# A two-layer mixer kernel: PSUM evictions issued half a state later, six state buffers in place of five, both halves of the step sizes in one PSUM slot

## The chip, the cores and the metric

The kernel runs on one core of one Trainium2 chip. A core has TensorE (PE in the profile; its weight loads are shown as PEld), VectorE (DVE), ScalarE (ACT), GpSimd (POOL) and SyncE (SP), which here issues the DMAs. The metric is the device time of one execution in microseconds; lower is better. The output must equal the reference's.

## The reference, cut to what matters

Two layers work on x of shape (4, 64, 64, 128). The costliest part is the selective scan of the first layer: four directions, 256 channels, 16 states for each channel, 4096 positions, four images.

```python
def step(h, xs):                       # over 4096 positions
    ut, dt, bt, ct = xs
    dA = jnp.exp(dt[..., None] * A)
    h = dA * h + (dt * ut)[..., None] * bt[:, :, None, :]
    y = jnp.einsum('bkdn,bkn->bkd', h, ct)
    return (h, y)
...
# layer 0
x = x + _L0_conv_ref(_ln_c(x), ...)    # projection, 3x3 convolution, selective scan, gate
t = t + _L0_ffn_ref(_ln_t(t), ...)     # 64 experts, each takes its top 8 positions
# layer 1
x = x + _L1_conv_ref(_ln_c(x), ...)    # self, row sum and column sum, three projections
t = t + _L1_ffn_ref(_ln_t(t), ...)     # long causal convolutions with 16 filters, and 3 taps
```

`dt` is softplus of a projection with rank 8, which the kernel calls the step sizes.

## The kernel before, in words

All data are fp32. The scan is cut into chunks: for each of 4 images and 4 directions, 8 chunks of 512 positions, 128 chunks in all. In a chunk each of the 16 states n is one step of the main loop, so there are 2048 steps s, each on tiles of 128 channels x 2 halves x 512 positions. The loop is software-pipelined. In step s of the program:

- SP loads the rows B and C of state s+5, spread over all partitions (`bc`, 6 buffers, L1355);
- ScalarE makes `da` = exp(dl * A) of state s+3, one instruction for each half (L1365, 5 buffers);
- VectorE makes `db` = du * B (L1392) and runs two scans into `hh` of state s (L1398, 5 buffers);
- GpSimd multiplies `hh` of state s-1 by C in place (L1408) and keeps the last column in `hst` (L1407);
- TensorE transposes `hh` of state s-2 into `y` and adds it up over the 16 states in PSUM (L1434, eight matmuls).

Once per chunk come the step sizes of the next chunk, `step_sizes`, one piece in each step from n = 1 on: load `dts` and `xc`; for each half take a PSUM tile `dt_ps`, project (L1280), and read it twice on ScalarE, into `ex` (L1282) and `dl` (L1283); then a softplus on ScalarE and GpSimd, which ends with `dl` (L1297) and `dx` = dl * x (L1299). At the end of the chunk ScalarE copies `dx` into PSUM as `du` (L1346), which has one buffer, so that the next chunk's `db` waits for this copy.

PSUM has 8 banks. `du`, `db` and `y` take 2 each; the last 2 are the side work's, either as two slots of one bank (`bank`, most of the time) or as one slot of two banks (`pair`, while `convolve` runs beside the recurrence; `bank` then takes half of it).

All other work of the kernel is side work, written as generators that yield a weight after each piece. Beside the recurrence of image b runs: for b = 0 the preparation of the other images, the gates and the filters' spectra; for b > 0 the end of the first layer for image b-1 (`after_scans`), the experts and the second layer's sums (`experts_and_sums`), the first transform of the long convolution (`to_slots`) and a part of the convolution itself (`convolve`: matmuls `cv_ps`, copied to SBUF as `y`, then 16 matmuls into `zq_ps`). `deal` takes pieces until their weights have reached what is due, twice in each step (in the middle and at the end of TensorE's transposes), except in the steps n = 2 and 3 of a chunk. It asks that the pieces' instructions come behind the step's own instruction on their engine. The final order on each engine is decided by a scheduler, which may move an instruction past others as long as dependencies and these requests hold. `pipelined` runs the stages of such a generator in the manner of a software pipeline: stage k of item g in the round g + k, an empty stage (None) is a round of waiting.

After the recurrence comes a tail: the side work of the last image together with most of the convolution, with all 8 banks as slots. There an eviction goes to VectorE and ScalarE in turn; beside the recurrence it is always a ScalarE copy (`evict`, L240).

Of the kernel before, what the change touches and what calls it, by code (L numbers as in the profile page):

```python
# [10 lines left out]
F32 = mybir.dt.float32  # L11
AF = mybir.ActivationFunctionType
# [5 lines left out]
P = 128  # L18
# [60 lines left out]
def kernel(  # L79
# [124 lines left out]

    side = {"tail": False}

    def slots(ones, twos):
        if "pool" in side:  # L210
# [2 lines left out]
        for name, n in (("ones", ones), ("twos", twos)):  # L213
            side[name] = n and side["pool"].enter_context(
                tc.tile_pool(name=f"side_{name}", bufs=n, space=PSUM)
            )

    def bank(shape, name):

        if side["ones"]:  # L220
            return side["ones"].tile(shape, F32, name=name, tag="ps")
        n = int(np.prod(shape[1:]))
        ap = pair(name)[0 : shape[0], 0, 0:n]
        if len(shape) == 2:
            return ap
        sizes = {f"d{i}": d for i, d in enumerate(shape[1:])}
        names = " ".join(sizes)
        return ap.rearrange(f"p ({names}) -> p {names}", **sizes)

    def pair(name):  # L230

        return side["twos"].tile([P, 2, 512], F32, name=name, tag="ps2")

    def evict(dst, src):
# [27 lines left out]
    def pipelined(n, *stages):  # L262


        for step in range(n + len(stages) - 1):
            for s in reversed(range(len(stages))):
                if 0 <= step - s < n and stages[s]:
                    stages[s][1](step - s)
                    yield stages[s][0]

    def norm_sums(pool, t, n, width, eps):

# [39 lines left out]
    def transposed(dst, src, n, name):  # L312

        ps = bank([P, n, P], name)
        for q in range(n):
            nc.tensor.transpose(ps[:, q, :], src[:, q, :], ident)
        evict(dst, ps.rearrange("c q p -> c (q p)"))

    def sigmoid_of(pool, ps, h):

# [14 lines left out]
    def before_scans(b):  # L335
# [6 lines left out]
        with tc.tile_pool(name="pa", bufs=1) as pa:  # L342
# [78 lines left out]
            with tc.tile_pool(name="pa_x", bufs=3) as px:  # L421
                xs, sts = {}, {}

                def load_x(i):
                    xs[i] = px.tile([P, 2, SC], F32, name="xc_x", bufs=5)
                    c = i % NSC
                    nc.sync.dma_start(
                        xs[i],
                        xc_d[b][i // NSC, :, :, c * SC : (c + 1) * SC].rearrange("h p l -> p h l"),
                    )  # L430

                def project(i):
# [6 lines left out]
                    evict(sts[i], ps)  # L439
# [12 lines left out]

                yield from pipelined(2 * NSC, (0.7, load_x), None, None, (1.8, project), None, (2.5, put_bc))
# [31 lines left out]
    def after_scans(b):  # L485

        with tc.tile_pool(name="po", bufs=2) as po:
# [19 lines left out]
            def add(g):  # L507
                ps = bank([P, 2, DI], "yk_ps")
                for k in range(K):
                    nc.tensor.matmul(ps, ident, yk.pop((g, k)), start=(k == 0), stop=(k == K - 1))  # L510
                y[g] = po.tile([P, 2, DI], F32, name="y", bufs=8)
                evict(y[g], ps)

            def sums(g):
                st[g] = norm_sums(po, y[g], 2, DI, eps5)
# [25 lines left out]
            def project(g):  # L541
                ps = bank([P, 2, C], "pr_ps")
                for q in range(2):
                    for h in range(2):
                        nc.tensor.matmul(
                            ps[:, q, :],
                            yT[g][:, h, q * P : (q + 1) * P],
                            w_out_t[:, h, :],
                            start=(h == 0),
                            stop=(h == 1),  # L550
                        )
                pr[g] = po.tile([P, 2, C], F32, name="pr")
                evict(pr[g], ps)

            yield from pipelined(
                16,
# [133 lines left out]
    def experts_and_sums(b):  # L690

        with tc.tile_pool(name="mk", bufs=1) as kp:
# [203 lines left out]
            with tc.tile_pool(name="l1", bufs=2) as lp:  # L896
# [4 lines left out]
                with tc.tile_pool(name="l1a", bufs=2) as la:  # L901
# [5 lines left out]
                    def scatter(g):  # L907
                        ps = bank([P, 4, C], "sc_ps")
                        for q in range(4):
                            t0 = 512 * g + q * P  # L910
                            nc.tensor.matmul(
                                ps[:, q, :], pT[:, t0 : t0 + P], outE, start=True, stop=True
                            )
                        sc[g] = la.tile([P, 4, C], F32, name="sc")
                        evict(sc[g], ps)

                    def sums(g):
                        st[g] = norm_sums(la, x4(g), 4, C, eps6)
# [32 lines left out]
                with tc.tile_pool(name="l1b", bufs=2) as lb:  # L951
# [5 lines left out]
                    def mix(g):  # L957
# [18 lines left out]
                        evict(zs[g], ps)  # L976

                    def sums2(g):
                        st2[g] = norm_sums(lb, x2g(g), 2, C, eps5)
# [15 lines left out]
                    def regress(g):  # L995
# [14 lines left out]
                        nc.scalar.activation(ar[g], ps, AF.Identity, scale=wseg[:, sg : sg + 1])  # L1010

                    yield from pipelined(
                        16,
# [21 lines left out]
    def to_slots(b):  # L1035

        with tc.tile_pool(name="fu", bufs=3) as fp:
            ub, uo = {}, {}

            def load(g):  # L1040

                ub[g] = fp.tile([NB, 4, 2, C], F32, name="ub")
                nc.sync.dma_start(
                    ub[g].rearrange("j t a c -> j (t a) c"),
                    u_d[b].rearrange("(j t) c -> j t c", j=NB)[:, 8 * g : 8 * g + 8, :],
                )

            def turn(g):
                uo[g] = fp.tile([P, 4, 2, C], F32, name="uo")
                for a in range(2):  # L1050
                    ps = bank([P, 4, C], "fu_ps")
                    nc.tensor.matmul(ps, fu_t, ub[g][:, :, a, :], start=True, stop=True)  # L1052
                    evict(uo[g][:, :, a, :], ps)

            def put(g):
                for r in range(2):
# [1 line left out]
                        ud[b][:, r, 4 * g : 4 * g + 4], uo[g][r * NQ : (r + 1) * NQ]  # L1058
                    )

            yield from pipelined(BS // 4, (0.5, load), (2.0, turn), (1.0, put))

    def convolve(groups, pool=None):

# [3 lines left out]
        with tc.tile_pool(name="cv", bufs=2) if pool is None else nullcontext(pool) as cp:  # L1068
# [30 lines left out]
            for i, (b, G, kq, e) in enumerate(parts):  # L1099
# [7 lines left out]
                for a in range(2):  # L1107

                    off = 1 - a if e == 1 else 0
                    for p in range(2):  # L1110
# [14 lines left out]
                                evict(to[:, q], pq[q])  # L1125
                            yield 0.0
                        else:
                            evict(to, ps)
                            yield 4.0
                if e == 0:  # L1130
                    continue
# [52 lines left out]
    def from_slots(b):  # L1184

        with tc.tile_pool(name="gi", bufs=3) as gp:
# [11 lines left out]
                    )  # L1198

            def turn(g):  # L1200
                xr[g] = gp.tile([NB, 4, 2, C], F32, name="xr3", bufs=4)
# [4 lines left out]
                iv[g] = gp.tile([NB, 4, 2, C], F32, name="iv")  # L1206
                for a in range(2):
                    ps = bank([NB, 4, C], "gi_ps")
                    nc.tensor.matmul(ps, gi_t, zb[g][:, :, a, :], start=True, stop=True)  # L1209
                    nc.scalar.activation(iv[g][:, :, a, :], ps, AF.Identity, scale=wpj[0:NB, :])  # L1210

            def add(g):

# [6 lines left out]
                    xr[g].rearrange("j t a c -> j (t a) c"),  # L1220
                )

            yield from pipelined(BS // 4, (0.7, load), (2.5, turn), (3.0, add), (0.5, put))

    def run(pieces):
        for _ in pieces:
# [23 lines left out]
    with ExitStack() as c0:  # L1250
# [11 lines left out]
        def step_sizes(b, k, ci):  # L1262


            dl = pb.tile([P, 2, SC], F32, name="dl", bufs=3)
            dx = pb.tile([P, 2, SC], F32, name="dx", bufs=1)
            xc = pb.tile([P, 2, SC], F32, name="xc")

            def pieces():
                cs = slice(ci * SC, (ci + 1) * SC)  # L1270
                dts = pb.tile([R, SC], F32, name="dts")
                nc.sync.dma_start(dts, dts_d[b][k, :, cs])
                nc.sync.dma_start(xc, xc_d[b][k % 2, :, :, cs].rearrange("h p l -> p h l"))
                yield
                ex = pb.tile([P, 2, SC], F32, name="ex", bufs=1)
                w = pb.tile([P, 2, SC], F32, name="w", bufs=1)

                for h in range(2):
                    ps = bank([P, SC], "dt_ps")
                    nc.tensor.matmul(ps, dtw[:, k, h * P : (h + 1) * P], dts, start=True, stop=True)  # L1280
                    bias = dtb[:, k, h : h + 1]
                    nc.scalar.activation(ex[:, h, :], ps, AF.Abs, bias=bias)  # L1282
                    nc.scalar.activation(dl[:, h, :], ps, AF.Relu, bias=bias)  # L1283
                    yield
                nc.scalar.activation(ex, ex, AF.Exp, scale=-1.0)
                yield
                nc.scalar.activation(w, ex, AF.Identity, bias=1.0)
# [28 lines left out]
        def deal(*behind):  # L1316


            if i % (K * NSC) < FIRST or s >= total or s % N in BUSY:
                return  # L1320
            start = len(traced)
            share["due"] += WEIGHT[chunks[i][0]] / ((K * NSC - FIRST) * (N - len(BUSY)) * 2)
            while share["made"] < share["due"]:
                share["made"] += next(share["pieces"], 1e9)
# [23 lines left out]
        for s in range(-5, total + 2):  # L1348
# [23 lines left out]
            if 0 <= s < total:  # L1372
                b, k, step, _ = chunks[i]
                n = s % N
                if n == 0:
                    if k == 0 and step == 0:
                        y_d[b] = dram.tile([K, L, DI], F32, name=f"y_d{b}")
                        if b > 0:
                            run(share["pieces"])
                        share = {"pieces": beside(b), "made": 0.0, "due": 0.0}  # L1380
                    hsts[i] = pb.tile([P, 2, N], F32, name="hst") if step == 0 else hsts[i - 1]
                    if i == 0:
                        into_psum(0)
                if i + 1 < len(chunks):
# [7 lines left out]
                nc.vector.tensor_mul(db, dus[i], bcs[s][:, 0:1, :].to_broadcast([P, 2, SC]))  # L1392
                for h in range(2):
# [183 lines left out]
```

## Time and profile before

| | us |
|---|---|
| median of three runs | 11290.32 (11284.48 to 11290.91) |
| the profiled execution | 11279.9 |
| its span, first to last instruction | 11278.1 |
| first `db` of the recurrence starts | 299.9 |
| last scan starts | 9087.1 |

| engine, busy in the span | us | share |
|---|---|---|
| TensorE matmuls | 8435.7 | 75% |
| VectorE | 8146.8 | 72% |
| GpSimd | 7262.7 | 64% |
| ScalarE | 6181.0 | 55% |

Costs of one instruction: `db` 1232 ns, a scan 1267 ns (1208 at the start of a direction), an exponential 716 ns, the product by C 2359 ns, a transposing matmul of `y` 322 ns as recorded (they overlap), a `dt_ps` matmul 822 ns. In the profile a name such as "hh<-da,hst,db" is output and inputs, L1398 the line; an idle time stands with the instruction that ended it. The shares of a whole span are averages over two quite different stages, so that the stretches have to be looked at one by one.

### The profile page before, as it was taken

The page shows a single profiled execution, that of the slowest core. Times are in us where ns is not written, and L with a number is a line of the kernel's source. Part 1 is how long each engine was busy: PE and PEld are TensorE (multiplying, and loading weights), DVE is VectorE, ACT ScalarE, POOL GpSimd, SP SyncE. Part 2 cuts the span into 40 slices and gives each one's busy share as a digit, 9 for nine tenths or more (in the row PEclk, how much of TensorE's full clock was granted, in tenths as well). Part 3 has the DMA queues.
Part 4 walks back from the last instruction along what each step waited for, and adds up shares of the span by engine and source line. Part 5 has one row for each costly group of instructions (what it writes and reads, how often), then busy time and mean ns, then how long its engine had stood idle before and what let it go on. Part 6 is the DMA issues. An engine that isn't in the chain of part 4 may idle for free. (4 is left out here: it accounts for less than half of the span.)

```text
span 11278.1 us, 117105 instructions
## 1 busy us (share of the span) xinstructions
PE 8435.7 (75%) x34656; PEld 4819.2 (43%) x34656; DVE 8146.8 (72%) x7046; ACT 6181.0 (55%) x12043; POOL 7262.7 (64%) x6518
## 2 busy tenths in 40 slices
PE   6677676556776777757766777576677789999998
PEld 2444443334453444444543344455344444355443
DVE  0898888887987999879878898798698932222222
ACT  4757575657466565664655566657455544124222
POOL 1888787888787877787867788888687821001001
PEclk9687787757777888878778788787788899999999
DMA  2565656566655666657565566575666664553555
GB/s 97 164 202 186 203 170 202 192 188 201 226 178 178 197 180 193 204 163 249 166 174 167 167 192 207 167 264 155 171 198 181 183 163 122 151 137 95 140 131 120
DMA packets 901457, 1980.14 MB, mean 176 GB/s; under 512 B 101562, under 2 KB 415578, under 8 KB 899290
## 3 DMA queue, kind: packets, MB, share of 16 engines
q1 hardware_dynamic: 900826, 1972.65, 58.2%
q8 instruction: 283, 4.64, 0.2%
q14 instruction: 348, 2.85, 0.1%
HBM read 1766.77 MB, written 205.52 MB: 175 GB/s over the span
## 5 line engine op out<-in xcount | busy, mean ns | idle before, releaser
L1408 POOL TENSOR_TENSOR hh<-hh,bc 128x1024 f32<-128x1024 f32 x2048 | 4829.8, 2359 | 434.2 <-DVE hh L1398 192.2
L1398 DVE TENSOR_TENSOR_SCAN hh<-da,hst,db 128x512 f32<-128x512 f32 x3584 | 4392.9, 1267 | 675.6 <-PE y L1434 297.9
L1365 ACT ACTIVATE da<-dl,aneg 128x512 f32<-128x512 f32 x4096 | 2766.3, 716 | 2084.4 <-DVE hh L1398 1998.3
L1434 PE MATMUL y<-ident,hh 128*128 128x128 f32 x16384 | 2808.2, 322 | 1214.8 <-POOL hh L1408 1095.7
L1434 PEld LDWEIGHTS y<-ident,hh 128*128 128x128 f32 x16384 | 2293.9, 167 | 2637.0 <-POOL hh L1408 1424.9
L1392 DVE TENSOR_TENSOR db<-du,bc 128x1024 f32<-128x1024 f32 x2048 | 2523.5, 1232 | 633.6 <-ACT du L1346 547.7
L1116 PE MATMUL cv_ps<-slab,us 64*128 64x512 f32 x4096 | 1197.3, 691 | 533.5 <-ACT y L240 277.8
L240 ACT COPY y<-cv_ps 128x512 f32<-128x512 f32 (+1 forms) x1024 | 754.3, 741 | 667.8 <-PE cv_ps L1116 638.0
L1407 POOL COPY hst<-hh 128x2 f32<-128x2 f32 x1792 | 338.9, 189 | 1123.6 <-DVE hh L1398 980.0
L1137 PE MATMUL zq_ps<-y,me 128*128 128x512 f32 x2048 | 1000.1, 609 | 49.0 <-ACT y L240 43.3
L1137 PE MATMUL zq_ps<-y,mo 128*128 128x512 f32 x2048 | 969.3, 597 | 0.0
L238 DVE COPY y<-cv_ps 128x512 f32<-128x512 f32 x640 | 441.5, 691 | 561.9 <-PE cv_ps L1116 511.8
L1116 PEld LDWEIGHTS cv_ps<-slab,us 64*128 64x128 f32 x4096 | 407.7, 206 | 1002.5 <-ACT y L240 369.3
L1153 POOL TENSOR_TENSOR zt<-zt,zt 128x512 f32<-128x512 f32 x64 | 81.2, 1268 | 996.2 <-DVE zt L238 536.5
L1398 DVE TENSOR_TENSOR_SCAN hh<-da,db 128x512 f32<-128x512 f32 x512 | 597.1, 1208 | 113.4 <-PE y L1434 70.8
L388 PE MATMUL cv_ps<-xh,diag 128*128 128x512 f32 x1152 | 534.7, 607 | 0.3 <-ACT xh L381 0.2
L1137 PEld LDWEIGHTS zq_ps<-y,me 128*128 128x128 f32 x2048 | 352.5, 193 | 382.2 <-issue 262.1
L1280 PE MATMUL dt_ps<-dts,dtw 8*128 8x512 f32 x512 | 371.4, 822 | 175.5 <-ACT dl L1283 48.3
L1137 PEld LDWEIGHTS zq_ps<-y,mo 128*128 128x128 f32 x2048 | 356.3, 191 | 316.6 <-issue 313.9
L1292 POOL TENSOR_TENSOR ex<-ex,dx 128x1024 f32<-128x1024 f32 x128 | 302.6, 2364 | 169.2 <-ACT dx L1289 169.0
L238 DVE COPY zt<-zq_ps 128x512 f32<-128x512 f32 x39 | 26.9, 691 | 529.0 <-PE zq_ps L1137 523.3
L510 PE MATMUL yk_ps<-yk,ident 128*128 128x512 f32 x512 | 275.2, 677 | 85.3 <-DMA yk<-y_d 34.0
(222 smaller groups left out, 8705.0 us busy)
## 6 DMA issues: line engine op xcount, KB each, us to landing
bc<-bc_d SPq DMA_DIRECT2D x2048, 512.0 KB
slab<-hd SPq DMA_DIRECT2D x1024, 256.0 KB
xc<-xc_d SPq DMA_DIRECT2D x128, 512.0 KB
y_d<-ys SPq DMA_DIRECT2D x128, 512.0 KB
w1t<-in_w_dram SPq DMA_DIRECT2D x128, 512.0 KB
w2t<-in_w_dram SPq DMA_DIRECT2D x256, 256.0 KB
xc_x<-xc_d SPq DMA_DIRECT2D x64, 512.0 KB
yk<-y_d SPq DMA_DIRECT2D x128, 256.0 KB
```

What stands on the lines that cost most here:

```text
L238: nc.vector.tensor_copy(dst, src)
L240: nc.scalar.copy(dst, src)
L388: nc.tensor.matmul(ps, diag[:, h, t, :], xh[:, 8 * g + dy : 8 * g + dy + 8, dx : dx + W], start=(t == 0), stop=(t == 8),)
L1116: nc.tensor.matmul(pq[q].rearrange("p (r k t) -> p r k t", r=2, t=BS), us[b, G][rows, p, a if e == 0 else 1 - a, :], slab[i][rows, p, :, : ...
L1137: nc.tensor.matmul(z, (me, mo)[e][:, KQ * kq + k, :], ys[e][:, :, :, :, k, :].rearrange("p a q r t -> p (a q r) t"), start=(e == 0 and k = ...
L1280: nc.tensor.matmul(ps, dtw[:, k, h * P : (h + 1) * P], dts, start=True, stop=True)
L1365: i_act = nc.scalar.activation(das[t][:, h, :], sizes[t // N][0][:, h, :], AF.Exp, scale=aneg[:, tk, h, t % N : t % N + 1],)
L1392: nc.vector.tensor_mul(db, dus[i], bcs[s][:, 0:1, :].to_broadcast([P, 2, SC]))
L1398: i_dve = nc.vector.tensor_tensor_scan(o, d0, d1, init, ALU.mult, ALU.add)
L1407: nc.gpsimd.tensor_copy(hsts[t // N][:, :, t % N], hhs[t][:, :, last])
L1408: i_pool = nc.gpsimd.tensor_mul(hhs[t], hhs[t], bcs.pop(t)[:, 1:2, :].to_broadcast([P, 2, SC]))
L1434: i_pe = nc.tensor.matmul(ys[c][:, q, h, :], hhs[t][:, h, q * P : (q + 1) * P], ident, is_transpose=True, start=(n == 0 and k > 0 and q % ...
```

## The change

Five edits.

- While the recurrence runs (`side["deals"]` is set), `evict_soon` doesn't issue the copy out of PSUM but puts it in a list, `soon`. `settle` issues what is in it: at the start of each `deal`, before a pair is taken, before the step sizes take their slot, at the end of a round of `pipelined` whose weights are under 6, and, all but the last, before a bank is taken. Ten kinds of eviction use it, among them those of `cv_ps`, `fu_ps`, `gi_ps`, `yk_ps`, `pr_ps`, `sc_ps`, `z_ps` and `ar_ps`; those of `zq_ps`, `zt_ps`, `pk_ps` and the reads of `cv_ps` in the first layer do not.
- `hh` has six buffers.
- While PSUM is a pair, both halves of `dt_ps` go to the two banks of one slot: two matmuls in one piece, four reads in the next.
- `to_slots` and `from_slots` get empty stages (between load and turn, turn and put, turn and add), and one buffer more for `ub`, `uo`, `iv` and `xr3`.
- `dl` has two buffers in place of three, `dts` one in place of two.

```diff
-    side = {"tail": False}
+    side = {"tail": False, "deals": False}
...
+    soon = []
+
+    def settle(leave=0):
+        while len(soon) > leave:
+            soon.pop(0)()
+
+    def evict_soon(work):
+        if side["deals"]:
+            soon.append(work)
+        else:
+            work()
+
     def bank(shape, name):

         if side["ones"]:
+            settle(1)
             return side["ones"].tile(shape, F32, name=name, tag="ps")
...
     def pair(name):

+        settle()
         return side["twos"].tile([P, 2, 512], F32, name=name, tag="ps2")
...
         for step in range(n + len(stages) - 1):
+            whole = 0.0
             for s in reversed(range(len(stages))):
                 if 0 <= step - s < n and stages[s]:
                     stages[s][1](step - s)
+                    whole += stages[s][0]
                     yield stages[s][0]
+
+            if whole < 6.0:
+                settle()
+        settle()
...
-        evict(dst, ps.rearrange("c q p -> c (q p)"))
+        evict_soon(lambda: evict(dst, ps.rearrange("c q p -> c (q p)")))
...
-                ub[g] = fp.tile([NB, 4, 2, C], F32, name="ub")
+                ub[g] = fp.tile([NB, 4, 2, C], F32, name="ub", bufs=4)
...
-                uo[g] = fp.tile([P, 4, 2, C], F32, name="uo")
+                uo[g] = fp.tile([P, 4, 2, C], F32, name="uo", bufs=4)
...
-                    evict(uo[g][:, :, a, :], ps)
+                    evict_soon(lambda ps=ps, a=a: evict(uo[g][:, :, a, :], ps))
...
-            yield from pipelined(BS // 4, (0.5, load), (2.0, turn), (1.0, put))
+            yield from pipelined(BS // 4, (0.5, load), None, (2.0, turn), None, (1.0, put))
...
-                            evict(to, ps)
+                            evict_soon(lambda to=to, ps=ps: evict(to, ps))
                             yield 4.0
...
-            yield from pipelined(BS // 4, (0.7, load), (2.5, turn), (3.0, add), (0.5, put))
+            yield from pipelined(BS // 4, (0.7, load), (2.5, turn), None, (3.0, add), (0.5, put))
...
-            dl = pb.tile([P, 2, SC], F32, name="dl", bufs=3)
+            dl = pb.tile([P, 2, SC], F32, name="dl")
...
-                dts = pb.tile([R, SC], F32, name="dts")
+                dts = pb.tile([R, SC], F32, name="dts", bufs=1)
...
-                for h in range(2):
-                    ps = bank([P, SC], "dt_ps")
+                settle()
+
+                def project(h, ps):
                     nc.tensor.matmul(ps, dtw[:, k, h * P : (h + 1) * P], dts, start=True, stop=True)
+
+                def read(h, ps):
                     bias = dtb[:, k, h : h + 1]
                     nc.scalar.activation(ex[:, h, :], ps, AF.Abs, bias=bias)
                     nc.scalar.activation(dl[:, h, :], ps, AF.Relu, bias=bias)
-                    yield
+
+                if side["ones"]:
+                    for h in range(2):
+                        ps = bank([P, SC], "dt_ps")
+                        project(h, ps)
+                        read(h, ps)
+                        yield
+                else:
+                    ps = pair("dt_ps")
+                    for work in (project, read):
+                        for h in range(2):
+                            work(h, ps[:, h])
+                        yield
...
             start = len(traced)
+            settle()
             share["due"] += WEIGHT[chunks[i][0]] / ((K * NSC - FIRST) * (N - len(BUSY)) * 2)
...
+        side["deals"] = True
...
                             run(share["pieces"])
+                            settle()
...
-                hhs[s] = pb.tile([P, 2, SC], F32, name="hh", bufs=5)
+                hhs[s] = pb.tile([P, 2, SC], F32, name="hh", bufs=6)
...
         run(share["pieces"])
+        settle()
+        side["deals"] = False
         side.pop("pool").close()
```

More of the change, by code (lines that the diff above doesn't have):

```diff
@@ L438, in project @@
                     sts[i] = px.tile([104, SC], F32, name="xd_st", bufs=4)
-                    evict(sts[i], ps)
+                    evict_soon(lambda: evict(sts[i], ps))
                 def put_bc(i):
@@ L511, in add @@
                 y[g] = po.tile([P, 2, DI], F32, name="y", bufs=8)
-                evict(y[g], ps)
+                evict_soon(lambda: evict(y[g], ps))
             def sums(g):
@@ L552, in project @@
                 pr[g] = po.tile([P, 2, C], F32, name="pr")
-                evict(pr[g], ps)
+                evict_soon(lambda: evict(pr[g], ps))
             yield from pipelined(
@@ L914, in scatter @@
                         sc[g] = la.tile([P, 4, C], F32, name="sc")
-                        evict(sc[g], ps)
+                        evict_soon(lambda: evict(sc[g], ps))
                     def sums(g):
@@ L975, in mix @@
                         zs[g] = lb.tile([P, 2, C], F32, name="zs")
-                        evict(zs[g], ps)
+                        evict_soon(lambda: evict(zs[g], ps))
                     def sums2(g):
@@ L1009, in regress @@
                         ar[g] = lb.tile([P, 2, C], F32, name="ar")
-                        nc.scalar.activation(ar[g], ps, AF.Identity, scale=wseg[:, sg : sg + 1])
+                        evict_soon(
+                            lambda: nc.scalar.activation(
+                                ar[g], ps, AF.Identity, scale=wseg[:, sg : sg + 1]
+                            )
+                        )
                     yield from pipelined(
@@ L1200, in turn @@
             def turn(g):
-                xr[g] = gp.tile([NB, 4, 2, C], F32, name="xr3", bufs=4)
+                xr[g] = gp.tile([NB, 4, 2, C], F32, name="xr3", bufs=5)
                 nc.sync.dma_start(
@@ L1205, in turn @@
                 )
-                iv[g] = gp.tile([NB, 4, 2, C], F32, name="iv")
+                iv[g] = gp.tile([NB, 4, 2, C], F32, name="iv", bufs=4)
                 for a in range(2):
@@ L1209, in turn @@
                     nc.tensor.matmul(ps, gi_t, zb[g][:, :, a, :], start=True, stop=True)
-                    nc.scalar.activation(iv[g][:, :, a, :], ps, AF.Identity, scale=wpj[0:NB, :])
+                    evict_soon(
+                        lambda ps=ps, a=a: nc.scalar.activation(
+                            iv[g][:, :, a, :], ps, AF.Identity, scale=wpj[0:NB, :]
+                        )
+                    )
             def add(g):
```

## The prediction

> **What bounds the kernel now.** I read the busy slices first, then the busy time by stretch, then VectorE's waits inside the long stage, then single waits in the timeline.
>
> ```profile
> PE   6677676556776777757766777576677789999998
> ...
> DVE  0898888887987999879878898798698932222222
> ...
> PEclk9687787757777888878778788787788899999999
> ...
> 300.00:2430.00 2130.00, 1432.55 (x5652) 893.47 (x5652) 1887.06 (x1557) 1376.30 (x2557) 1760.29 (x1386) 0.75 0.58 188
> ...
> 9088.00:11278.00 2190.00, 2113.19 (x7106) 942.18 (x7104) 541.68 (x781) 688.87 (x1625) 260.75 (x532) 0.98 0.54 132
> ```
>
> Two regimes: from 300 to 9088 us the recurrence runs with VectorE the busiest (1887 of 2130 us in its first quarter, the columns being PE, weight loads, DVE, ACT, POOL); the last 2190 us are TensorE's, 2113 busy. The floor of the first regime is one state on VectorE:
>
> ```profile
> 6268.81 2.45 DVE L1398 TENSOR_TENSOR_SCAN hh<-da,hst,db 128x512 f32<-128x512 f32 x2
> 6271.29 1.23 DVE L1392 TENSOR_TENSOR db<-du,bc 128x1024 f32<-128x1024 f32 x1
> 6272.66 2.45 DVE L1398 TENSOR_TENSOR_SCAN hh<-da,hst,db 128x512 f32<-128x512 f32 x2
> ```
>
> Scans of one state start 3.85 us after those of the state before. 2048 x 3.85 = 7885 us, but the stage takes 8788, so some 900 us are lost. About 100 of them are other VectorE work (maxima, sums); the rest is waiting, and one view names it:
>
> ```profile
> DVE db L1392 <- ACT du L1346: 547.7, 50, 289.5
> DVE hh L1398 <- PE y L1434: 368.7, 115, 17.5
> DVE hh L1398 <- ACT da L1365: 56.8, 31, 5.7
> ...
> PE cv_ps L1116 <- ACT y L240: 262.5, 158, 8.6
> ...
> PE fu_ps L1052 <- DMA ub<-u_d: 55.3, 7, 20.1
> ...
> PE dt_ps L1280 <- ACT dl L1283: 48.3, 32, 10.9
> ```
>
> (total us, times, longest.) The 289.5 is the start-up; the other 258 us of du fall at chunk boundaries. The second line is a full ring of hh tiles: scan s cannot write until TensorE has transposed state s-5. The last three are why TensorE is late: it stands before a PSUM slot that ScalarE has not emptied, or a late load. One boundary shows it whole:
>
> ```profile
> 6267.66 0.60 PE L1434 MATMUL y<-ident,hh 128*128 128x128 f32 x4
> 6273.15 2.07 PE L1280 MATMUL dt_ps<-dts,dtw 8*128 8x512 f32 x2 [4.89 <-ACT zt L240]
> 6276.57 2.07 PE L1280 MATMUL dt_ps<-dts,dtw 8*128 8x512 f32 x2 [1.36 <-DMA slab<-hd]
> 6280.00 2.15 PE L1116 MATMUL cv_ps<-slab,us 64*128 64x512 f32 x4 [1.36 <-DMA bc<-bc_d]
> 6282.08 1.97 PE L1434 MATMUL y<-ident,hh 128*128 128x128 f32 x8
> ...
> 6302.39 1.23 DVE L1392 TENSOR_TENSOR db<-du,bc 128x1024 f32<-128x1024 f32 x1 [11.84 <-ACT du L1346]
> ```
>
> dt_ps waits for zt's eviction, the second half for both reads of the first, the convolution for the reads of the second; no transpose of the recurrence starts for 14 us. (The DMA names are misattributed: both matmuls follow the end of a dl read by 0.05 us.)
>
> **What the Trainium skill says.** "PSUM — Partial Sum Buffer", section Engine vs sequencer instructions: the queues of ScalarE, VectorE and GpSimd are strict FIFO and matmuls start in program order. The lines above agree: transposes whose hh was ready sat behind dt_ps. "Perfetto Trace Analysis", section Optimization Strategy: a repeated gap on the engine that should be full can mean too few buffers for the next tile. The 115 hh waits agree in kind. "TensorE: Matmul & The Clock Gate", section HAM oscillation: idle gaps over about 3.4 us put TensorE back to half clock. The trace agrees: four fu_ps records take 3.75 us after a 9.42 us wait and 1.98 us in a stretch without one; so a TensorE wait taken away also makes the next work faster.
>
> **The change, part by part**, against the profiled execution (11279.9 us; span 11278.1), which lies 10 us under the median 11290.3.
>
> *Sixth hh tile.* It lets VectorE run one state further ahead of TensorE. A stretch of late TensorE then costs one state, 3.85 us, less, once per stretch, as the ring must refill in between. I followed each VectorE wait over 0.15 us back to its cause: 405 us belong to transposes (some under other names than the 368.7), in 74 stretches when waits at most five states apart are put together. Capped at 3.85 each they sum to 192 us. Not all comes back: where TensorE stays late until the chunk ends, du is late next, and where ScalarE is the pace (norm phases: the 16 states from 2726 us take 92 us instead of 61.7, ScalarE 73 of them busy, and the scans wait for da) the time is due anyway. I take 60%: 115 us; bounds 40 and 192.
>
> *Evictions half a state later.* No instruction is added; a copy keeps its 0.57 to 1.0 us. On ScalarE it now stands in the next deal's place. The orders of the two programs, compared engine by engine, show how little that is: a scheduler had already moved the evictions behind later exponentials; 153 of some 2050 state groups differ on TensorE, 19 on VectorE, 750 on ScalarE, mostly by one place or one state, and the neighbours of du are the same at half of the boundaries. Gain: ScalarE no longer stands at a matmul not yet done (164 us before cv_ps copies in the stage) while exponentials queue behind it; those have four states in hand, so little reaches VectorE. Loss: the PSUM slot is held longer, by up to two exponentials (2 x 0.716 = 1.43 us), and TensorE's next side matmul, the transposes behind it and then hh wait. On time, the exponentials of a state end about 1.4 us after the scan that frees them and a pair's copy 1.0 later, 2.4 us; TensorE reaches its slot after POOL's 2.36 us product and four transposes, about 3 us. So it just fits. Net +10 us of gain; bounds -150 and +40.
>
> *Both halves of dt in one slot.* Only where PSUM is one pair (the convolution's 48 chunks). It removes the wait between the halves: 1.36 us in the lines above, 48.3 us in all on TensorE, and brings the second dt one or two states forward in 38 of them. In eight slow chunks (80 to 87) dt stands behind a whole zq sum, is not moved, and du is late by up to 11.8 us; there the dl chain gains about 1.35 us each, 11 us. Elsewhere most of it is hidden by the sixth tile: 6 us. Together 17; bounds 0 and 60.
>
> *Loads two steps ahead in to_slots.* The SP queue had ud stores, which wait for evictions, ahead of later ub loads (6 stores held it 11.4 us at 5717). Now four ub loads go first. Of 55 us of ub waits the first of each of three runs stays, about 35; 15 of the rest reach VectorE. Bounds 0 and 40.
>
> *dl 3 to 2, dts 2 to 1 buffers.* The old dl has been read ten states before it is rewritten, dts almost a chunk before: 0.
>
> *du.* Where VectorE no longer stops for hh, it reaches the chunk's end with TensorE later than before, and a du behind an eviction is then late: I give back 27 us (bounds 0 and 80), the next wait in line.
>
> *Tail.* Evictions are immediate there, the matmuls the same in number and TensorE 96% busy: 0, within 15.
>
> Sum: 115 + 10 + 17 + 15 - 27 = 130 us. 11279.9 - 130 = 11150 for that execution, 11160 for the median.
>
> **Rivals.**
> *The reordering does little and the sixth tile hands over to du (15%).* For: half the du neighbours are unchanged and 258 us of du already wait. Against: after nearly all long hh waits near a chunk's end no du wait follows. Time: 192 x 0.2 = 38 less du's 27: about 11280.
> *The gains chain (8%).* TensorE, interrupted less, stays at full clock (0.75 to 0.80 now), its lateness vanishes and all 405 us less the 150 of rate-bound stretches go: 11290 - 255 = 11035.
> *Slower: the held slot (17%).* In the convolution one pair serves every cv_ps, dt_ps and zq sum. Of 384 pair evictions half are issued at a state's end and now fall behind the next two exponentials: 192 x 1.43 = 275 us of TensorE time. It decides from the point where ScalarE reaches an eviction later than TensorE its slot, by the above with only 0.6 us of margin; then TensorE's lateness exceeds what one more hh tile (3.85 us per stretch) hides, and the gains of 130 shrink to the other phases' half. 11290 + 275 - 65 - a third of the 275 hidden (92) = about 11410. For: TensorE already waits 262.5 us for y copies. Against: where TensorE is late the exponentials have already been run.
>
> **How the numbers follow.** 60% for the forecast, 11160, its own range 11080 to 11235. Faster by over 0.2% (23 us, about what a measurement here tells from none): 0.60 + 0.08 + 0.06 of the first rival = 0.74; within: 0.09; slower: 0.17. The range 11040 to 11340 leaves out a third of the chained case and most of the upper half of the slower one.
>
> **What would show it.** Waits of the scan for y: from 368.7 to about 250, fewer than 70; TensorE's dt_ps wait for dl in the convolution gone; du (without start-up) at 230 to 290; ub waits near 35; chunks of the second convolution nearer 61.7 us; 9088 moves to about 8960 and the tail stays near 2190. Wrong if cv_ps's wait for y copies grows past 400 us, or the hh waits stay above 330.

## The result, and the profile after

| | before | after |
|---|---|---|
| median (runs) | 11289.81 us (4) | 11197.33 us (4; 11189.8 to 11203.89) |
| ratio after / before, 95% interval | | 0.992 [0.9907, 0.9932] |
| profiled execution | 11279.9 us | 11189.8 us |
| first `db` to the end of the last scan | 299.9 to 9088.3 | 297.0 to 9007.2 |
| from there to the end of the span | 2189.8 us | 2180.8 us |

The change makes the kernel 92 us faster, most of it in the recurrence (78 us of the 90 between the two profiled executions; the tail is 9 us shorter). Busy slices of the page, and busy time in its first quarter and in the tail (columns as before: PE, weight loads, DVE, ACT, POOL, clock, DMA share, GB/s):

```profile
PE   6677676546766777657677776576677789999999
...
DVE  0898988887887999879878898798699933222222
...
PEclk9787777757776888778778887687788899999999
...
300.00:2430.00 2130.00, 1406.59 (x5652) 882.42 (x5650) 1886.03 (x1557) 1375.90 (x2556) 1762.08 (x1387) 0.75 0.58 189
9008.00:11188.00 2180.00, 2111.85 (x7100) 940.43 (x7100) 541.18 (x780) 688.77 (x1625) 260.09 (x532) 0.99 0.53 133
```

The picture has the same two regimes, and VectorE is as busy in the first quarter as it was (1886 against 1887 us): its work is unchanged, and its waits must have gone. The waits of VectorE and then of TensorE between 300 and 9030 us (total us, times, longest) show which:

```profile
DVE db L1440 <- ACT du L1393: 340.6, 55, 16.8
DVE hh L1446 <- PE y L1482: 176.3, 49, 19.8
DVE hh L1446 <- ACT da L1412: 79.5, 40, 6.3
...
DVE db L1440 <- DMA bc<-bc_d: 34.7, 23, 7.9
...
PE cv_ps L1142 <- ACT y L256: 284.9, 166, 8.7
...
PE fu_ps L1078 <- DMA ub<-u_d: 43.0, 3, 19.3
```

The window leaves out the start-up, so that 340.6 stands against 258 of before. The full ring of hh cost 368.7 us and now costs 176.3: 192 us less. But du rose by 82 us, da by 23 and bc by 22 (from 12.6 us in 6 waits). Some 127 of the 192 us have changed their name and are still paid. The order of the first two lines has turned round.

By stretch: the convolution's 48 chunks went from 3120.2 to 3069.5 us, the other chunks with side work of b > 0 from 3534.1 to 3505.9, those of the first image not at all (2134.2 and 2134.7).

The boundary that the prediction showed lies here in the changed kernel (timelines of TensorE, ScalarE, GpSimd and VectorE; start, duration):

```profile
6220.06 3.78 PE L1311 MATMUL dt_ps<-dts,dtw 8*128 8x512 f32 x4 [4.89 <-ACT zt L256]
6226.35 2.15 PE L1142 MATMUL cv_ps<-slab,us 64*128 64x512 f32 x4 [2.51 <-ACT dl L1316]
...
6242.04 1.33 ACT L1412 ACTIVATE da<-dl,aneg 128x512 f32<-128x512 f32 x2 [8.67 <-POOL dl L1342]
6243.28 0.99 ACT L256 COPY y<-cv_ps 128x1024 f32<-128x1024 f32 x1
6244.17 2.56 ACT L1412 ACTIVATE da<-dl,aneg 128x512 f32<-128x512 f32 x4
6246.63 0.99 ACT L256 COPY y<-cv_ps 128x1024 f32<-128x1024 f32 x1
6247.53 0.59 ACT L1393 COPY du<-dx 128x512 f32<-128x512 f32 x1
6248.05 0.72 ACT L1412 ACTIVATE da<-dl,aneg 128x512 f32<-128x512 f32 x1
6248.67 0.58 ACT L1393 COPY du<-dx 128x512 f32<-128x512 f32 x1
...
6242.09 2.35 POOL L1344 TENSOR_TENSOR dx<-dl,xc 128x1024 f32<-128x1024 f32 x1
...
6249.28 1.23 DVE L1440 TENSOR_TENSOR db<-du,bc 128x1024 f32<-128x1024 f32 x1 [11.87 <-ACT du L1393]
```

The two halves of the step sizes now stand together on TensorE (four matmuls in 3.78 us), and yet the boundary takes as long as it did: from the first `dt_ps` to the first `db` it is 29.2 us in both kernels, and `db` waits 11.87 us against 11.84. Two things make `du` late here. GpSimd ends `dx`, which `du` is a copy of, only at 6244.44, when VectorE has already waited for 7.0 us: that is the chain of the step sizes. From then on the copy stands in ScalarE's queue for 3.1 us more: before `du`, ScalarE works through seven exponentials of the *new* chunk (six, then one between the halves) and two evictions. The late `dx` is peculiar to the boundaries into chunks 81 to 88, which hold 68 of the 341 us of du (47 before); at every other du wait over 4 us `dx` had long been ready.

### The profile page after: what moved, and what is told of

It reads as the page before. It is cut to its first block, busy times and chain, and to the rows that moved or that the text cites. A ratio compares the mean times of both kernels' runs of the same rounds, so it can differ in the third digit from the quotient of the medians.

```text
span 11188.0 us, 117102 instructions
## 1 busy us (share of the span) xinstructions
PE 8372.3 (75%) x34656; PEld 4820.6 (43%) x34656; DVE 8145.9 (73%) x7046; ACT 6173.9 (55%) x12043; POOL 7262.3 (65%) x6518
## 5 line engine op out<-in xcount | busy, mean ns | idle before, releaser
L1142 PE MATMUL cv_ps<-slab,us 64*128 64x512 f32 x4096 | 1164.0, 674 | 528.0 <-ACT y L256 298.5
```

What stands on the lines that cost most here:

```text
L1142: nc.tensor.matmul(pq[q].rearrange("p (r k t) -> p r k t", r=2, t=BS), us[b, G][rows, p, a if e == 0 else 1 - a, :], slab[i][rows, p, :, : ...
```

## The experiments

Three theories were set against one another. *Theory 1*: the sixth hh tile is the gain, and much of it is handed to the next wait, du, whose copy has no slack at the chunk's end. *Theory 2*: something other than the tile carries the gain, or the lateness is TensorE's and only changes its name. *Theory 3*: the tile brings more and another part of the change, or a contention, takes some back. Each expectation says what they mean in its run. Each ratio is to the kernel before, timed beside the kernel of the row. Medians of the kernel before lie between 11280 and 11292 us in these comparisons, so that a difference of medians in different comparisons is given with that of the ratios. "Waits" are VectorE's between 300 and 9030 us in the profiled execution, without the start-up.

| kernel | median us | ratio to before [95%] | waits for y | waits for du |
|---|---|---|---|---|
| before | | | 368.7 | 258 |
| after | 11197.33 | 0.992 [0.9907, 0.9932] | 176.3 | 340.6 |
| a_hh5 | 11264.84 | 0.9984 [0.9978, 0.9991] | 329.6 | 269.2 |
| b_hh6 | 11212.09 | 0.9938 [0.9926, 0.9951] | 205.4 | 354.3 |
| a_nodefer | 11178.76 | 0.9906 [0.9891, 0.9921] | 191.1 | 338.9 |
| a_dtsplit | 11197.46 | 0.9924 [0.9911, 0.9936] | 176.3 | 346.2 |
| a_noslots | 11210.32 | 0.9934 [0.9922, 0.9947] | 224.3 | 340.7 |
| a_defer_only | 11277.75 | 0.9997 [0.9989, 1.0006] | 328.0 | 260.5 |
| a_hh7 | 11185.77 | 0.9909 [0.9893, 0.9926] | 118.6 | 384.3 |
| a_du0 | 11128.37 | 0.9862 [0.9848, 0.9875] | 195.6 | 138.0 |
| a_du0_hh5 | 11221.69 | 0.9947 [0.9934, 0.9961] | 389.0 | 88.9 |
| n_du0 | 11116.60 | 0.9853 [0.9839, 0.9866] | 205.4 | 158.5 |
| n_front | 11126.18 | 0.9863 [0.985, 0.9877] | 193.7 | 255.3 |
| n_front_du0 | 11106.08 | 0.9846 [0.9833, 0.986] | 212.0 | 97.4 |

### The sixth tile taken away, and alone

```diff
-                hhs[s] = pb.tile([P, 2, SC], F32, name="hh", bufs=6)
+                hhs[s] = pb.tile([P, 2, SC], F32, name="hh", bufs=5)
```

> The changed kernel with five hh tiles again; all else of the change stays. Theory 1 (the sixth tile carries the gain, and hands part of it to du): 60 to 110 us slower than the changed kernel, so within 35 us of the kernel before; the scan's waits for y go from 176 back to 320 or more, the waits of db for du fall from 341 to below 290. Theory 2 (the deferred evictions carry the gain, the sixth tile is only used up by what they hold longer): at most 30 us slower than the changed kernel, waits for y below 230. Theory 3 (the sixth tile brings its full 192 us and the deferral takes 100 of them away): 150 us or more slower than the changed kernel, that is, 60 us slower than the kernel before.

The reverse in the kernel before, with two `dl` and one `dts` to make room:

```diff
-                hhs[s] = pb.tile([P, 2, SC], F32, name="hh", bufs=5)
+                hhs[s] = pb.tile([P, 2, SC], F32, name="hh", bufs=6)
```

> The kernel before with six hh tiles (and, for room, two dl and one dts); no other part of the change. Theory 1: 50 to 90 us faster than the kernel before; waits for y near 190, waits for du up by 60 to 90 from 258 without the start-up. Theory 2: at most 30 us faster. Theory 3: 150 us faster or more, with du no higher than before.

Without the tile the changed kernel is 67 us slower (72 by the ratios); with the tile alone the kernel before is 71 us faster. VectorE's waits of a_hh5, then of b_hh6:

```profile
DVE hh L1446 <- PE y L1482: 329.6, 100, 18.6
DVE db L1440 <- ACT du L1393: 269.2, 49, 16.7
```

```profile
DVE db L1392 <- ACT du L1346: 354.3, 60, 15.4
DVE hh L1398 <- PE y L1434: 205.4, 40, 15.8
DVE hh L1398 <- ACT da L1365: 69.7, 34, 7.5
DVE db L1392 <- DMA bc<-bc_d: 43.1, 19, 8.1
```

The tile takes 153 to 163 us from the y waits in either direction and adds 71 to 96 to du and 28 to 31 to bc. That is Theory 1 in both runs, though du rose in the second a little more than the 60 to 90 us expected. The rest of the change together is worth some 20 us (11282.9, the kernel before in that comparison, to 11264.8).

### The deferral undone, and alone

```diff
     def evict_soon(work):
-        if side["deals"]:
-            soon.append(work)
-        else:
-            work()
+        work()
```

> The changed kernel in which each eviction is issued at once, as before; six hh tiles, the step sizes in one slot and the empty stages stay. Theory 1: within 15 us of the changed kernel. Theory 2: 50 us or more slower than it. Theory 3 (a held slot costs TensorE time): 50 us or more faster than it, and TensorE's waits before cv_ps for y copies fall below 262 us from 285.

a_defer_only is the changed kernel with the five-tile line above, the step sizes of a_dtsplit and the `to_slots` of a_noslots (both below).

> The changed kernel with five hh tiles, the step sizes half by half and no empty stages in to_slots: what is left of the change is the deferral of evictions alone (with the empty stages of from_slots and the smaller dl and dts). Theory 1 (deferral costs some 15 us, as undoing it showed): 5 to 25 us slower than the kernel before. Theory 2 (deferral helps with five tiles, as the prediction's +10 had it): 5 to 20 us faster.

Undoing it gave 18.6 us, 16 by the ratios: just outside the 15 of Theory 1, in the direction of Theory 3 but far less than its 50, and the two intervals overlap. Alone it did nothing that can be told from zero (0.9997 [0.9989, 1.0006]), so neither side of that expectation was met. The held slot is not a large effect: TensorE's waits before `cv_ps` for y copies are 284.9 us with the deferral and 270.5 without it. The interval of a_defer_only leaves room for a gain of 12 us at most.

The profiled executions, one of each kernel, point to a cost. In a_defer_only the recurrence took 8803 us against 8788 before, 15 us more; its tail was 14 us shorter, but the tail is where evictions are issued at once and where the new `from_slots` runs. With six tiles the recurrence took 8710 us with the deferral and 8698 without it (a_nodefer). So no pair of runs shows a gain from the deferral; a cost of some 12 to 15 us in the recurrence is likely, and not shown beyond the noise.

### The step sizes half by half

```diff
-                if side["ones"]:
-                    for h in range(2):
-                        ps = bank([P, SC], "dt_ps")
-                        project(h, ps)
-                        read(h, ps)
-                        yield
-                else:
-                    ps = pair("dt_ps")
-                    for work in (project, read):
-                        for h in range(2):
-                            work(h, ps[:, h])
-                        yield
+                for h in range(2):
+                    ps = bank([P, SC], "dt_ps")
+                    project(h, ps)
+                    read(h, ps)
+                    yield
```

> The changed kernel in which each half of the step sizes takes its own turn of the slot, as before. Theory 1: the pair of halves is worth its 17 us of the prediction, between 5 and 40, all of it in the convolution's 48 chunks, and TensorE's dt_ps waits for dl rise from 31 to about 48 us; if the sixth tile already hides it, within 5 us. Theory 2 says nothing other. Theory 3 (a pair taken for both halves is held through four reads and delays the next cv_ps): 10 us or more faster than the changed kernel.

No difference by the medians (11197.46 and 11197.33 us), 5 us by the ratios, whose intervals overlap, although TensorE's `dt_ps` waits for dl rise from 30.6 to 53.1 us as expected. In the convolution's chunks they are 21.6 us before, none after, and 21.4 us here. A wait of TensorE went, and nothing that can be told from zero came of it.

### The empty stages of to_slots taken out

```diff
-            yield from pipelined(BS // 4, (0.5, load), None, (2.0, turn), None, (1.0, put))
+            yield from pipelined(BS // 4, (0.5, load), (2.0, turn), (1.0, put))
```

> The changed kernel without the empty stages in to_slots, so that a load of ub is one round ahead of its use again. Theory 1 (the stages bring what chunks 46, 79, 110 and 111 lost to late loads): 15 to 40 us slower than the changed kernel, fu_ps waits for ub rise from 43 to 55 us or more, and those four chunks together rise from 344 to about 375 us. Theory 2 (the sixth tile alone shortened those chunks): within 8 us of the changed kernel, the four chunks stay near 344 us.

13 us slower, 16 by the ratios, whose intervals overlap. TensorE's waits for ub rise from 43.0 to 53.9 us, and chunks 46, 79, 110 and 111 together from 344.0 to 357.4 us (380.5 before). The size and the place agree with Theory 1 in part: most of what those chunks gained since before (23 of 36 us) they keep without the stages.

### A seventh tile

```diff
-                hhs[s] = pb.tile([P, 2, SC], F32, name="hh", bufs=6)
+                hhs[s] = pb.tile([P, 2, SC], F32, name="hh", bufs=7)
```

> The changed kernel with seven hh tiles; for their room to_slots has no empty stages and some buffers of side work are fewer (ub and uo 3, xr 7, ex1's pool 7, u 3, uT 2, the small no_ tiles 4), all outside the convolution's 48 chunks. It is read beside the kernel without those stages and with six tiles (11210.3 us; y waits 224, du 341). Theory 1 (each further tile hides one more state of a late stretch, and its gain is again handed to du): in the convolution's chunks and those of the first image the y waits, 30 and 40 us there, halve, du rises by about as much, and these stretches (3071 and 2138 us) shorten by at most 20 us together; the whole within 30 us of 11210. Theory 2 (lateness is only buffered away): 40 us or more faster than 11210, with du no higher.

VectorE's waits of a_hh7, from 305 us on:

```profile
DVE db L1440 <- ACT du L1393: 384.3, 60, 16.7
DVE hh L1446 <- PE y L1482: 118.6, 28, 11.8
DVE hh L1446 <- ACT da L1412: 84.7, 40, 6.3
DVE db L1440 <- DMA bc<-bc_d: 66.3, 32, 8.9
```

Against a_noslots y falls by 106 us, du rises by 44 and bc by 32; by the ratios (0.9934 and 0.9909, overlapping intervals) the kernel gains some 28 us. The convolution's chunks and those of the first image shorten from 3071.1 to 3060.9 and from 2137.7 to 2128.2 us, 20 us together, at the edge of what Theory 1 allowed. There du rose by only 4 us and bc by 10, less than it said. In the whole kernel the series of five, six and seven tiles is plain: y 328, 224, 119 us and du 260, 341, 384 us (a_defer_only, a_noslots, a_hh7; the first has the step sizes half by half too, and the last fewer side buffers).

### One state of slack for du

`dx` in SBUF holds what `du` in PSUM will hold. Of the changed kernel's du waits over 4 us, at all but those of chunks 81 to 88 it was ready at least 18 us before the copy ended.

```diff
-                nc.vector.tensor_mul(db, dus[i], bcs[s][:, 0:1, :].to_broadcast([P, 2, SC]))
+                du = sizes[i][1] if n == 0 else dus[i]
+                nc.vector.tensor_mul(db, du, bcs[s][:, 0:1, :].to_broadcast([P, 2, SC]))
```

> The changed kernel in which the first db of a chunk reads dx in SBUF, of equal content, in place of the copy du in PSUM; the copy has one state (3.85 us) more time. Theory 1 (what hh gained was handed to du, because the copy has no slack): the 55 waits for du, each shortened by at most 3.85 us, lose 174 of their 341 us; about half of it reaches the end, so 60 to 110 us faster than the changed kernel. Theory 2 (TensorE is late in any case and the wait only changes its name): at most 25 us faster, the scan's waits for y rise by 100 or more. Theory 3 (an operand of db in SBUF is read slower or collides with GpSimd): db of these 128 states takes 1.5 us or more in place of 1.23, and the gain shrinks by 128 times the difference.

> The same kernel with five hh tiles. Theory 1: the sixth tile is worth more where du has slack: this kernel is 80 to 130 us slower than the one with six, against 67 us without that slack (11264.8 less 11197.3 to 11198). Theory 2: the sixth tile is worth 67 us or less here.

The same edit beside evictions issued at once:

> The changed kernel with evictions issued at once and with the first db of a chunk reading dx. Theory 1: the two edits add up: 10 to 25 us faster than the one with dx and deferred evictions, and faster than both kernels of the case by 75 us or more. If the 15 us that undoing the deferral showed were chance, within 5 us of that kernel.

a_du0 is 69 us faster than the changed kernel: du falls by 203 us, 31 us of waits for `dx` come in its place, and y rises by 19 where Theory 2 had 100. The sixth tile is now worth 93 us (11221.7 less 11128.4; 96 by the ratios) in place of 67 (72). Both agree with Theory 1: the du wait had been eating a part of the tile's gain. That the tile's worth rose is less certain than the 69 us: by the intervals, 96 and 72 are known to some 20 and 15 us. n_du0 is another 12 us below, with overlapping intervals, as for the deferral above.

Theory 3 is right as well in its collision. The first `db` of a chunk took 1769 ns on the mean in place of 1233, which is 68 us over 127 chunks; how much of them reaches the end no run shows. Timelines of VectorE and GpSimd in a_du0 at one boundary:

```profile
7410.26 3.14 DVE L1441 TENSOR_TENSOR db<-dx,bc 128x1024 f32<-128x1024 f32 x1
7413.54 1.28 DVE L1447 TENSOR_TENSOR_SCAN hh<-da,hst,db 128x512 f32<-128x512 f32 x1
...
7409.96 2.35 POOL L1457 TENSOR_TENSOR hh<-hh,bc 128x1024 f32<-128x1024 f32 x1
7412.25 1.19 POOL L1456 COPY hst<-hh 128x2 f32<-128x2 f32 x1
```

`db` starts while GpSimd's product runs, which ends at 7412.31; `db` ends 1.09 us after that. The copy `hst` behind it, about 0.2 us elsewhere, takes 1.19 us: now GpSimd is held by `db`.

### du ahead of the new chunk's exponentials

In the programs' order ScalarE had eight exponentials (four states) of the new chunk ahead of the first `du` at 91 of 127 boundaries, as they were ready earlier. Here the block that issues `da`, which stood ahead of the copy, follows it in the program (that move is left out below), and from the third state of a new chunk on it is queued behind it. Evictions are issued at once in this kernel:

```diff
-                    into_psum(i + 1)
+                    last_du = into_psum(i + 1)
...
+                    if s >= 0 and t // N > i and t % N >= 2:
+                        tc.add_manual_dep(i_act.ins, last_du.ins.name, order, reason="queued behind")
```

> The changed kernel with evictions issued at once, in which the exponentials of the third state of a new chunk, and so all side work dealt after them, are queued behind the copy du; before, ScalarE ran eight exponentials of the new chunk ahead of du at 91 of 127 boundaries. Theory 1 (du is late because of what stands ahead of it on ScalarE): du comes up to four exponentials (4 times 0.65 us) earlier; the waits for du fall from 339 to 240 us or less, and the kernel is 30 to 80 us faster than the 11178.8 of its parent. Theory 2 (ScalarE then stands at du for the last db of the old chunk, and evictions and TensorE are late in its place): du's waits fall but the scan's waits for y and da rise by as much; within 20 us of the parent, or slower.

Waits of VectorE, and of ScalarE before `du`, in n_front:

```profile
DVE db L1426 <- ACT du L1390: 255.3, 47, 13.6
DVE hh L1432 <- PE y L1482: 193.7, 45, 20.6
DVE hh L1432 <- ACT da L1441: 94.0, 35, 9.5
...
ACT du L1390 <- DVE db L1426: 388.8, 71, 7.7
```

53 us faster than a_nodefer. du falls by 84 us, a little less than expected, y stays (191 to 194) and da rises by 25. ScalarE now stands 389 us before `du` for the last `db` of the old chunk, which no line showed before, and TensorE's waits before `cv_ps` for y copies rise from 270.5 to 315.5 us; what Theory 2 feared is there and costs far less than the edit brings. So the order on ScalarE was a cause of du's lateness: four exponentials now stand ahead of `du` at all 127 boundaries. The 53 us belong to both parts of the edit, as the move of the block was not tried by itself. It is no remedy for a late `dx`: at the boundaries into chunks 81 to 88 du still costs 60 us, against 64 in a_nodefer.

> Both edits at the boundary: the copy du ahead of the third state's exponentials, and the first db of a chunk from dx. Theory 1: the two cut the same waits, so less than their sum: 10 to 50 us faster than the 11116.6 of the kernel with dx alone. Theory 2: within 15 us of 11116.6.

Both edits: 11106.1 us, the fastest kernel measured, 0.9846 [0.9833, 0.986] of before. Apart they brought 53 us (order) and 62 us (dx) against a_nodefer, together 73: they cut the same wait. The 10 us that the order adds to dx lie in the ranges of both theories and within what the intervals can't tell apart.

## Why the prediction was right, and where its sum was off

The forecast of 11160 us was right in its direction and its main cause; 130 us were foretold and 92 came.

- *Sixth tile, 115, and du, -27.* The mechanism was right: a sixth tile shortens the waits for y, and du takes a part of it back. Both sizes were off, and the errors offset each other. Of the y waits 115 us were counted; 192 went, in the change as a whole, and 153 to 163 by the tile itself, and 49 waits were left where fewer than 70 were foretold. (That 192 is also the capped sum is chance: the sum was made from 405 us of waits, some under other names.) The weakest step is the give-back. It was sized at 27 us with an upper bound of 80; du rose by 82 us in the change, by 71 in a_hh5 against after and by 96 in b_hh6, and stands at 341 us where 230 to 290 were foretold. bc and da, not in the sum, took 28 and 11 more (a_hh5 against after). Net, the tile brought 67 to 71 us where these two terms made 88; that they came so near is in part luck. The evidence read was that "after nearly all long hh waits near a chunk's end no du wait follows". It was true of a kernel in which VectorE arrived late because of those very waits. Where du rose, it rose by 102 us together, 67 of them at boundaries behind a chunk that had lost waits for y. The copy that VectorE then meets was just in time before: at 91 boundaries of either kernel eight exponentials stood ahead of it, and at eight its `dx` comes late.
- *Evictions half a state later, +10.* Alone 0.9997 [0.9989, 1.0006], that is 3 us faster, give or take 10: right that it is small, but no run shows the gain, and in the recurrence by itself the profiled executions show 12 to 15 us of loss. The rival of the held slot at -275 us is excluded: `cv_ps` waits for y copies reached 285 us, far from its 400.
- *Both halves of dt, +17.* Nothing that can be told from zero. The 48.3 us of TensorE's waits were read as the convolution's; only 21.6 of them, in 19 waits, lie in its chunks. Those went, as foretold, but the 11 us that the slow chunks were to gain weren't there. At the boundary shown, the four reads on ScalarE end 6.24 us after the first matmul starts in place of 6.80, so the edit saves 0.56 us and not 1.35, since the first half's reads now wait for both halves. And GpSimd's next step of the chain (`ex` minus `dx`) starts 12.31 us after that matmul in both kernels: a product of the recurrence ran ahead of it in both, and the 0.56 us went into waiting for its end. As the prediction quoted the Trainium skill, "PSUM — Partial Sum Buffer", section Engine vs sequencer instructions, GpSimd's queue is strictly in order; it was applied to TensorE and not to the third engine of the dl chain.
- *to_slots, +15.* 13 us measured, 16 by the ratios, with overlapping intervals; ub waits at 43.0 us where 35 were foretold.
- *Tail, 0 within 15.* It is 9 us shorter. In the eleven other kernels with the new `from_slots` it is 2175.6 to 2183.1 us, in b_hh6 without it 2189.7; of the change's parts only those of `from_slots` (its empty stage, and a buffer more for `iv` and `xr3`) divide them so. They were not tried by themselves.
- *The sum.* With what was measured in place of each term: tile and du 67 to 71, deferral 0 to -15, dt 0, to_slots 13 to 16, tail 9. That makes 74 to 96 us, and 92 came. The recurrence ends at 9007 us, where 8960 were foretold.
- *The chained gain.* TensorE's clock in the first quarter is 0.75 as before: no chain there. That a wait taken away makes the next work faster was drawn from two `fu_ps` timings; it does not hold everywhere. In the kernel before, after a wait of 12.07 us, the granted clock stood at 0.50 from 7930 to 7970 us, though TensorE was busy for 39.7 of these 40 us.
- *Convolution.* Its second pass (chunks 80 to 95) was to come nearer to 61.7 us a chunk. It went from 66.9 to 66.1: db still waits up to 11.9 us for du there, where `dx` itself is late, and no part of the change brought `dx` forward.

## What to carry to other kernels

In this kernel a deeper ring took off the wait that it is named for, and the next fixed appointment of the same engine decided how much arrived: 44% (67 of 153 us). Before counting a wait as gained, list what the engine meets next once it is on time, and how much slack each of these has: what its input is waiting for, and the order in front of it on its own engine. "It isn't late now" is no evidence. Then try to give the slack as well: an order of two copies was worth 53 us here, and with a state of slack for `du` the same tile seemed worth more (93 us in place of 67).

## What the runs showed of the hardware

- VectorE's product with both inputs in SBUF and a GpSimd instruction shut each other out. In a_du0, 44 of 127 such `db` took over 1.4 us; in all 44 a GpSimd instruction was running at the start, and 41 of them ended 1.09 us after it. The other way round, 72 `hst` copies that started during such a `db` took 1.15 to 1.24 us in place of 0.2 and ended 0.04 us after it. With `du` in PSUM the same `db` takes 1233 ns on the mean (n_front), and never over 1.4 us, though GpSimd was running at the start of 106 of the 127. The Trainium skill, "SBUF — State Buffer", section SBUF: two separate sides, has it so: an exclusive lock held for the whole instruction, which a VectorE instruction with two SBUF inputs needs against a GpSimd one that reads SBUF. The trace agrees, and shows what the two PSUM banks of `du` save.
- Of the other three, one stretched to 14.24 us while twelve GpSimd instructions started one after another (14.19 us in n_du0 and 14.37 us in n_front_du0 at the same place): waiting did not give VectorE the next turn.
